# Mamba layer, then attention with experts, on one core: an earlier second front, late gates bridged by the pair's last outputs, and the net's norms and sums moved off VectorE

## The chip, the cores and the metric

One NeuronCore of a Trainium2 chip runs the whole program. The metric is the time of one execution on the device in microseconds (us), as a median over runs. The core's engines are TensorE (PE; its weight loads are listed as PEld), VectorE (DVE), ScalarE (ACT), GpSimd (POOL) and SyncE (SP). Each works through its own instructions in order, and they wait for one another through semaphores. DMAs are issued from SP and from POOL. A DMA that adds to its destination is issued from POOL here.

## The reference

The input is x, 8 sequences of 512 positions and 256 features, all in float32. Two layers follow each other:

```python
x = x + layernorm(mamba(layernorm(x)))
x = x + layernorm(ffn(layernorm(x)))

# mamba: 512 inner channels, 16 states
xs, z = split(x @ in_proj_w.T)
xc = silu(causal_conv4(xs) + conv_b)
dt_r, B, C = split(xc @ x_proj_w.T)
dt = softplus(dt_r * dt_proj_w + dt_proj_b)
h_t = exp(dt_t * A) * h_(t-1) + dt_t * B_t * xc_t        # along the sequence
y = sum over states of h * C + xc * D
return (y * silu(z)) @ out_proj_w.T

# ffn: 16 heads of width 64; 8 experts, the best 2 of each head are kept, for values and for outputs
q, k = rope(x @ Wq), rope(x @ Wk)
gv, go = gates(x, Wsel_v), gates(x, Wsel_o)              # sigmoid, top 2 of 8
v = sum_e gv_e * (x @ Wv_e);  o = softmax(q k^T / 8) @ v
src = x + sum_e go_e * (o @ Wo_e)
y = ln(src) * ln1_g + ln1_b
y = y + relu(y @ W1 + b1) @ W2 + b2
return ln(y) * ln2_g + ln2_b
```

## The kernel before

The 8 sequences, b = 0 to 7, are a pipeline. For each there are four pieces of work, written as Python generators:

- `front(b)` normalizes x, projects it, makes the convolution on VectorE (`xs`, one `tensor_scalar` and three `scalar_tensor_tensor` for each of four channel blocks), applies Silu, projects to B, C and dt, writes the gate `sz` to DRAM, and makes the softplus in pieces: `u` = exp(-|.|), `ln` = log(1 + u), and a correction that uses `w` = (1 + u) - 1, where VectorE takes u - w and adds it to `ln`. At its end b is in `prepared`.
- `mamba(b)` makes `dt` and `dtx`, then 32 scan steps. A step is a product `h<-bt,dtx`, a `tensor_tensor_scan` `h<-da,h`, and a product `h<-h,ct`, all on 128x1024, on VectorE. ScalarE makes the decay `da` of the next step in one of two buffers (`decays`), and two adding DMAs from POOL sum h into `xc` (`xc<-h`). After the scan come `xc*sz`, the output projection `ps_out`, two norms (`x1`, `xn`), the transposes `ps_tr_g`, the gate logits `ps_sel` and the first half of the gates, `best(0, gv)`. Now b is in `state`.
- `heads(b)` makes the second half of the gates, `best(1, gt)`, and writes it to DRAM (`ps_go`). Now b is in `gated`.
- `feed_forward(b)` is what the change calls the net: residual, norm, W1, Relu, W2, two norms, output.

The attention of a sequence is an order written out by hand in `ahead`, for 8 pairs of heads. For a pair there are values `ps_v` (with gates applied on VectorE and added up on POOL as `ve`), scores `ps_s`, transposes `ps_pt` and the sum `ps_o`. The eight output steps of the pair before, `last.add_output(0..7)` (matmuls `ps_a`), are spread between these. Late in each pair `follow` projects the next pair's q and k (`ps_qk`); VectorE then makes `sin` and `qk`, and four small adding DMAs from POOL (`qk<-sin`) complete the rotation that the first `ps_s` needs. At a pair 7, `follow` runs the planner until b + 1 is in `state`.

`_Order` is the planner. It keeps a clock for PE and one for VectorE, and holds the running generators with a rank; a lower rank goes first. A generator's part is emitted when VectorE's planned clock is behind PE's. A `yield` gives the estimated time until the next part can run. The planner only fixes the order in which each engine meets its instructions. `_Vector` records every VectorE instruction, so they all carry line 160 in the profile.

PSUM has three tiles of two banks for everything (`banks`) and one for the sum `ps_a`. SBUF pools `big` (7 buffers) and `half` (5) hold the temporary tiles.

Lines that matter: front(1) is started by mamba(0) with rank `FIRST` = 0.2, behind mamba(0)'s own rank 0, and holds before its convolution until `through` has 0:

```python
            while b == 1 and 0 not in through:
                yield 1.0
...
                order_of.start(front(b + 1), 2 * b - 1 if b else FIRST)
```

In the net, each half of the hidden layer is made as two tiles of two halves. TensorE makes one half, ScalarE applies Relu to it, then TensorE makes the other half of the same tile.

Of the kernel before, what the change touches and what calls it, by code (L numbers as in the profile page):

```python
# [37 lines left out]
NG = 2  # L38
# [14 lines left out]
NET, FIRST = -9, 0.2  # L53
# [8 lines left out]
class _Norm:  # L62
# [7 lines left out]
    def __call__(self, out, rows):  # L70

        nc, vector, n = self.nc, self.vector, len(rows)
        st = self.pool.tile([P, n, 6], F32, tag="ln_st", name="ln_st")
        mv = self.pool.tile([P, n, 2], F32, tag="ln_mv", name="ln_mv")
        rs = self.pool.tile([P, n], F32, tag="ln_rs", name="ln_rs")
        for i, r in enumerate(rows):
            vector.bn_stats(st[:, i, :], r)
            vector.bn_aggr(mv[:, i, :], st[:, i, :])
            yield 0.0
        vector.tensor_scalar(rs, mv[:, :, 1], EPS, None, ALU.add)  # L80
        nc.gpsimd.tensor_tensor(rs, rs, self.power[:, :n], ALU.pow)
        yield 1.5
        for i, r in enumerate(rows):
            vector.tensor_scalar(
                out[:, i, :], r, mv[:, i, 0:1], rs[:, i : i + 1], ALU.subtract, ALU.mult
            )
            yield 0.1
# [113 lines left out]
def _layers(  # L201
# [4 lines left out]
    with ExitStack() as ctx:  # L206
# [18 lines left out]
        sz_d = [tc.dram_tile([NC // 2, P, 2, S], F32, name=f"sz_d_{b}") for b in range(B)]  # L225
        wqk_d = [tc.dram_tile([P, 2, ND, P], F32, name=f"wqk_d_{i}") for i in range(H // 2)]
# [9 lines left out]
        rows_t = const.tile([P, 4, D], F32, name="rows_t")  # L236
        g1, o1, g2, o2 = (rows_t[:, i : i + 1, :].to_broadcast([P, NT, D]) for i in range(4))
# [12 lines left out]
        def later_constants():  # L250
# [5 lines left out]
            nc.sync.dma_start(out=b1_t, in_=b1)  # L256
            nc.sync.dma_start(
                out=rows_t.rearrange("p r d -> p (r d)"),
                in_=rows[:, : 4 * D].to_broadcast([P, 4 * D]),
            )  # L260
            yield 8.0

# [31 lines left out]
        def front(b):  # L294
# [43 lines left out]
            while b == 1 and 0 not in through:  # L338
                yield 1.0
# [51 lines left out]
            for u in us:  # L391
# [5 lines left out]
                for i in range(2):  # L397
                    w = half.tile([P, S], F32, tag="half", name=f"w_{b}_{m + i}")
                    vector.tensor_scalar(w, u[:, i, :], 1.0, 1.0, ALU.add, ALU.subtract)
                    yield 0.0  # L400
                    vector.tensor_tensor(u[:, i, :], u[:, i, :], w, ALU.subtract)
                    yield 0.0
                vector.tensor_tensor(ln, ln, u, ALU.add)
# [9 lines left out]
        def mamba(b):  # L413
# [3 lines left out]
            xs, lns, row = prepared[b]  # L417
            dt = one.tile([P, NC, S], F32, tag="dt", name=f"dt_{b}")
# [5 lines left out]
            for m in range(0, NC, 2):  # L424
# [4 lines left out]
                yield 0.1  # L429
            while b and b - 1 not in through:  # L430
# [5 lines left out]

            def decays(k):
                g, m = k // NC * NG, k % NC
                for j in range(NG):
                    nc.scalar.activation(  # L440
                        das[k % 2][:, j, 1:S], dt[:, m, 1:S], AF.Exp,
                        scale=decay[:, m, g + j : g + j + 1],
                    )
# [7 lines left out]
            if b + 1 < B:  # L451
                order_of.start(front(b + 1), 2 * b - 1 if b else FIRST)
                order_of.start(mamba(b + 1), 2 * (b + 1))
            steps = NS // NG * NC
            decays(0)
# [33 lines left out]
            while 0 < b < B - 1 and b + 1 not in prepared:  # L489
# [322 lines left out]
        def feed_forward(b, pa):  # L812

            xt, _ = state.pop(b)
            acc = big.tile([P, ND, S], F32, tag="big", name=f"acc_{b}")
            vector.tensor_tensor(acc, xt, pa, ALU.add)
            summed.add(b)
            yield 0.1
# [11 lines left out]
            yield from norm(y, [y[:, t, :] for t in range(NT)])  # L830
            vector.tensor_tensor(y, y, g1, ALU.mult)
            yield 0.0
            vector.tensor_tensor(y, y, o1, ALU.add)
            yield 0.1
            yt = big.tile([P, ND, S], F32, tag="big", name=f"yt_{b}")
            to_features(yt, y, f"f_{b}")
            pe(1.05)
            yield 1.2
            b2 = half.tile([P, 1, D], F32, tag="half", name=f"b2_{b}")
            nc.sync.dma_start(out=b2[:, 0, :], in_=rows[:, 4 * D :].to_broadcast([P, D]))  # L840
            vector.tensor_tensor(y, y, b2.to_broadcast([P, NT, D]), ALU.add)

            for k in range(2):
# [3 lines left out]
                for f in range(0, NF // 2, 2):  # L847
                    ps = banks(f"ps_f1_{b}_{k}_{f}")
                    h = big.tile([P, 2, S], F32, tag="big", name=f"hid_{b}_{k}_{f}")
                    for i in range(2):  # L850
                        at = k * NF // 2 + f + i
# [5 lines left out]
                        pe(1.71)  # L857
# [17 lines left out]
                yield 0.1  # L875
                vector.tensor_tensor(y, y, ps, ALU.add)
                yield 4.0
            z = big.tile([P, NT, D], F32, tag="big", name=f"z_{b}")
            x1 = big.tile([P, NT, D], F32, tag="big", name=f"x1_f_{b}")
            nc.sync.dma_start(out=x1, in_=x1_d[b])  # L880
            yield from norm(z, [y[:, t, :] for t in range(NT)])
# [4 lines left out]
            yield from norm(z, [z[:, t, :] for t in range(NT)])  # L886
            vector.tensor_tensor(z, z, x1, ALU.add)
# [9 lines left out]
        def follow(b, pair):  # L897

            b, pair = (b, pair + 1) if pair + 1 < H // 2 else (b + 1, 0)
            if b < B:  # L900
                order_of.run(lambda: b in state)
# [20 lines left out]
        with tc.manual_schedule(engines=MANUAL):  # L922
# [9 lines left out]
            for b in range(B):  # L932
                for pair in range(H // 2):
                    now = pairs.pop((b, pair))
                    ahead(now, lambda: follow(b, pair))
                    if pair == 0 and b:
# [5 lines left out]
            for k in range(E):  # L942
                last.add_output(k)
                order_of.run()
            order_of.start(feed_forward(B - 1, sums[B - 1]), NET)
# [84 lines left out]
```

## Time and profile before

| what | value |
|---|---|
| median of 3 runs (lowest to highest) | 3809.67 us (3799.65 to 3812.99) |
| the profiled execution: its time, its span | 3804.05 us, 3802.3 us |
| mean granted TensorE clock | 0.942 |
| busy in the span: PE, DVE, ACT, POOL | 88%, 80%, 44%, 44% |
| bytes moved by DMA | 584.19 MB, mean 154 GB/s |
| shares of the chain that ended last | PE 57%, DVE 21%, DMA 7%, ACT 6%, issue 6%, POOL 3% |

The profile is of one execution. "Busy" is the share of the span in which an engine had an instruction in work. The chain that ended last is followed back from the last instruction to what released it. Idle time of an engine that is not the bottleneck costs nothing. In a group of instructions, the columns are busy time and mean duration, then the idle time of that engine just before them and what ended it.

### The profile page before, as it was taken

How to read it: one execution, taken by the hardware profiler on the slowest of the kernel's cores; microseconds unless marked ns; L12 is line 12 of the kernel's file. 1: busy time of each engine (PE TensorE's matmuls, PEld its weight loads, DVE VectorE, ACT ScalarE, POOL GpSimd, SP SyncE). 2: the span in 40 equal slices, each digit the busy share in tenths (PEclk: the TensorE clock that was granted, in tenths of full speed). 3: DMA queues.
4: the chain of work that ended last, by engine and by line, in shares of the span. 5: the costliest groups of instructions: out<-in, count | busy, mean ns of one | idle time of the engine just before them, and what ended most of it. 6: DMA issues, size and time to landing. Idle time of an engine off the chain costs nothing.

```text
span 3802.3 us, 33611 instructions
## 1 busy us (share of the span) xinstructions
PE 3362.9 (88%) x10464; PEld 1560.0 (41%) x10464; DVE 3049.0 (80%) x3218; ACT 1657.2 (44%) x2761; POOL 1656.8 (44%) x1601
## 2 busy tenths in 40 slices
PE   2039999399989999999999999999999999999996
PEld 0023444244444444444444444444444444444443
DVE  6976899799879888799878988799888989664432
ACT  4216654144544446444563446334463435332331
POOL 1323466255534545345443554445453557332220
PEclk6569999699999999999999999999999999999998
DMA  5934778368755867468674877557683777443431
GB/s 164 202 63 128 176 188 194 84 168 192 179 146 139 189 168 192 119 160 195 160 187 106 195 173 190 141 145 187 162 208 91 182 193 180 116 111 101 120 94 56
DMA packets 287760, 584.19 MB, mean 154 GB/s; under 512 B 37848, under 2 KB 125144, under 8 KB 287584
## 3 DMA queue, kind: packets, MB, share of 16 engines
q1 hardware_dynamic: 205664, 431.00, 38.3%
q0 software_dynamic: 81920, 151.04, 24.5%
q8 instruction: 85, 1.39, 0.1%
q14 instruction: 91, 0.75, 0.1%
HBM read 409.39 MB, written 21.51 MB: 113 GB/s over the span
## 4 chain that ended last, share of the span: by engine, by line
PE 57%; DVE 21%; DMA 7%; ACT 6%; issue 6%; POOL 3%; SPq 0%; DVEq 0%; POOLq 0%; ACTq 0%
PE ps_a L803 16%; PE ps_v L735 14%; DVE h L160 8%; PE ps_s L676 5%; PE ps_o L764 3%; PE ps_pt L711 3%; PE ps_f L853 3%; DMA xc<-h 3%; PE ps_qk L638 3%; PE ps_f L868 3%; DVE og L160 2%; DMA qk<-sin 2%; DVE ve L160 2%; PE ps_out L511 2%; DVE low L160 1%
## 5 line engine op out<-in xcount | busy, mean ns | idle before, releaser
L750 POOL TENSOR_TENSOR ve<-ve 128x512 f32<-128x512 f32 x256 | 420.2, 1641 | 1348.6 <-DVE ve L160 1248.0
L803 PE MATMUL ps_a<-og,wo 128*128 128x512 f32 x2048 | 978.5, 617 | 11.6 <-DVE og L160 11.2
L735 PE MATMUL ps_v<-wv,xt 128*128 128x512 f32 x2048 | 935.2, 599 | 3.8 <-ACT p L691 3.8
L160 DVE TENSOR_TENSOR_SCAN h<-da,h 128x1024 f32<-128x1024 f32 x256 | 609.7, 2382 | 87.1 <-ACT da L440 74.5
L691 ACT ACTIVATE p<-ps_s,low 128x512 f32<-128x512 f32 x512 | 347.3, 683 | 708.2 <-DVE low L160 707.7
L448 POOL DMA_DIRECT2D xc<-h x512 | 493.3, 1168 | 360.0 <-DMA xc<-h 145.6
L803 PEld LDWEIGHTS ps_a<-og,wo 128*128 128x128 f32 x2048 | 378.7, 195 | 547.4 <-issue 471.9
L735 PEld LDWEIGHTS ps_v<-wv,xt 128*128 128x128 f32 x2048 | 380.5, 191 | 517.0 <-issue 472.8
L700 ACT ACTIVATE p<-p,total 128x512 f32<-128x512 f32 x512 | 341.2, 714 | 190.5 <-DVE total L160 190.5
L160 DVE TENSOR_TENSOR og<-o,gb 128x1024 f32<-128x1024 f32 x256 | 311.6, 1238 | 118.2 <-ACT o L770 49.5
L160 DVE TENSOR_TENSOR ve<-ps_v,gv 128x1024 f32<-128x1024 f32 x256 | 311.4, 1216 | 117.4 <-PE ps_v L735 113.6
L717 ACT COPY pt<-ps_pt 128x1024 f32<-128x1024 f32 x256 | 256.7, 1003 | 334.8 <-PE ps_pt L711 334.1
L676 PE MATMUL ps_s<-qk 64*128 64x512 f32 x1024 | 328.8, 660 | 82.4 <-DMA qk<-sin 60.1
L440 ACT ACTIVATE da<-dt,decay 128x511 f32<-128x511 f32 x512 | 337.6, 713 | 140.9 <-DVE h L160 140.4
L160 DVE TENSOR_TENSOR h<-bt,dtx 128x1024 f32<-128x1024 f32 x256 | 345.1, 1348 | 17.6 <-DMA xc<-h 17.3
L160 DVE TENSOR_REDUCE low<-ps_s 128x2 f32<-128x1024 f32 x256 | 310.8, 1214 | 56.8 <-PE ps_s L676 55.9
L160 DVE TENSOR_TENSOR h<-h,ct 128x1024 f32<-128x1024 f32 x256 | 326.2, 1274 | 3.6
L751 POOL TENSOR_TENSOR ve<-ve 128x256 f32<-128x256 f32 x256 | 308.1, 1203 | 20.2
L660 POOL DMA_DIRECT2D qk<-sin x256 | 207.9, 1258 | 214.1 <-DVE qk L160 85.1
L711 PEld LDWEIGHTS ps_pt<-ident,p 128*128 128x128 f32 x2048 | 240.2, 142 | 133.9 <-issue 106.3
L711 PE MATMUL ps_pt<-ident,p 128*128 128x128 f32 x2048 | 267.5, 274 | 6.2 <-ACT pt L717 6.1
L511 PE MATMUL ps_out<-w_out,xc 128*128 128x256 f32 x256 | 66.5, 422 | 213.5 <-DVE xc L160 211.6
(114 smaller groups left out, 3271.9 us busy)
## 6 DMA issues: line engine op xcount, KB each, us to landing
xc<-h POOLq DMA_DIRECT2D x512, 256.0 KB, 5.7
gb<-go_d SPq DMA_DIRECT2D x512, 256.0 KB, 5.0
wv<-in_wv_dram SPq DMA_DIRECT2D x128, 512.0 KB, 4.6
wo<-in_wo_dram SPq DMA_DIRECT2D x512, 128.0 KB, 3.6
bt<-bc_d SPq DMA_DIRECT2D x64, 512.0 KB, 6.2
ct<-bc_d SPq DMA_DIRECT2D x64, 512.0 KB, 7.1
wqk<-wqk_d SPq DMA_DIRECT2D x64, 256.0 KB, 2.6
qk<-sin POOLq DMA_DIRECT2D x256, 64.0 KB, 4.4
```

Source lines behind the costliest of these rows:

```text
L160: return getattr(self.engine, name)(*args, **kw)
L440: nc.scalar.activation(das[k % 2][:, j, 1:S], dt[:, m, 1:S], AF.Exp, scale=decay[:, m, g + j : g + j + 1],)
L448: nc.gpsimd.dma_start(out=xc[:, k % NC, :], in_=h[:, j, :], accum_op=ALU.add)
L676: nc.tensor.matmul(ps[:, j, :], lhsT=self.qk[feats, 0, bass.ts(t, P)], rhs=self.qk[feats, 1, :], start=True, stop=True,)
L691: nc.scalar.activation(p[:, j, :], ps[:, j, :], AF.Exp, bias=low[:, j : j + 1], accum_out=total[:, j : j + 1],)
L700: nc.scalar.mul(p[:, j, :], p[:, j, :], total[:, j : j + 1])
L711: nc.tensor.transpose(pp[:, j, bass.ts(i, P)], self.p[t][:, j, bass.ts(i, P)], ident)
L717: nc.scalar.copy(self.pt[:, :, :, bass.ts(t, P)], pp.rearrange("p j (i q) -> p j i q", q=P))
L735: nc.tensor.matmul(ps[:, i, :], lhsT=self.xt[:, c, bass.ts(t + i, P)], rhs=self.wv[:, c, :], start=(c == 0), stop=(c == ND - 1),)
L750: nc.gpsimd.tensor_tensor(ve[:, :, 0:4], ve[:, :, 0:4], ve[:, :, 4:8], ALU.add)
L751: nc.gpsimd.tensor_tensor(ve[:, :, 0:2], ve[:, :, 0:2], ve[:, :, 2:4], ALU.add)
L803: nc.tensor.matmul(pa[:, c, :], lhsT=self.wo[:, i, bass.ts(c, P)], rhs=self.og[q][:, i, :], start=(self.pair == 0 and k == 0), stop=(self. ...
```

## The change

It has five parts.

1. **The second front.** front(1) is started with rank -1, before mamba(0)'s 0, and no longer waits for `through`. mamba(0) waits after its scan until front(1) is prepared, as the others did. The first decays of a sequence, `decays(0)`, are emitted right after dt and dtx and ahead of the wait for `through`.
2. **Late gates.** `follow` no longer runs the planner until b + 1 is in `state`; if it isn't, nothing is projected. After pair 7 is attended, and if pair 0 of b + 1 has not been projected, the eight output steps of pair 7 are emitted at once, with a try of `follow` after each. The net of b starts then, and pair 0 of b + 1 has no output steps between its parts.
3. **The net's norms.** ScalarE applies them as scale * x + offset, with one small VectorE instruction for the offset. The softplus's `w` = 1 + u is also made on ScalarE, and VectorE does one `scalar_tensor_tensor` in place of two instructions.
4. **The net's sums.** ScalarE copies out of PSUM, and an adding DMA from POOL adds: the residual, b2 (together with ln1_b, laid out in DRAM at the start), both halves of W2's product, and x1 at the end. ln1_b's own addition goes into the copy of `yt` as ScalarE's bias.
5. **Relu.** Both halves of a hidden tile are made before ScalarE applies Relu to the two.

```diff
-    def __call__(self, out, rows):
+    def __call__(self, out, rows, scalar=None):
...
+        if scalar:
+            off = self.pool.tile([P, n], F32, tag="ln_off", name="ln_off")
+            vector.scalar_tensor_tensor(off, mv[:, :, 0], -1.0, rs, ALU.mult, ALU.mult)
+            yield 0.1
+            for i, r in enumerate(rows):
+                scalar.activation(
+                    out[:, i, :], r, AF.Identity, scale=rs[:, i : i + 1], bias=off[:, i : i + 1]
+                )
+                yield 0.5
+            return
...
-            while b == 1 and 0 not in through:
-                yield 1.0
...
-                    vector.tensor_scalar(w, u[:, i, :], 1.0, 1.0, ALU.add, ALU.subtract)
+                    nc.scalar.activation(w, u[:, i, :], AF.Identity, bias=1.0)
+                    yield 0.9
+                    vector.scalar_tensor_tensor(
+                        u[:, i, :], w, -1.0, u[:, i, :], ALU.add, ALU.subtract
+                    )
                     yield 0.0
-                    vector.tensor_tensor(u[:, i, :], u[:, i, :], w, ALU.subtract)
-                    yield 0.0
-                vector.tensor_tensor(ln, ln, u, ALU.add)
+                vector.tensor_tensor(ln, ln, u, ALU.subtract)
...
+            decays(0)
             while b and b - 1 not in through:
                 yield 0.5
...
-                order_of.start(front(b + 1), 2 * b - 1 if b else FIRST)
+                order_of.start(front(b + 1), 2 * b - 1)
...
-            while 0 < b < B - 1 and b + 1 not in prepared:
+            while b + 1 < B and b + 1 not in prepared:
                 yield 0.5
...
         def feed_forward(b, pa):
+            def add_to(t, what):
+                nc.gpsimd.dma_start(out=t, in_=what, accum_op=ALU.add)
...
-            vector.tensor_tensor(acc, xt, pa, ALU.add)
+            nc.scalar.copy(acc, pa)
+            yield 1.2
+            add_to(acc, xt)
...
-            yield from norm(y, [y[:, t, :] for t in range(NT)])
+            yield from norm(y, [y[:, t, :] for t in range(NT)], nc.scalar)
             vector.tensor_tensor(y, y, g1, ALU.mult)
-            vector.tensor_tensor(y, y, o1, ALU.add)
...
+            for c in range(ND):
+                nc.scalar.activation(yt[:, c, :], ps[:, c, :], AF.Identity, bias=o1[:, c : c + 1])
+            add_to(y, ob_d.rearrange("o t d -> o (t d)").to_broadcast([P, NT * D]))
...
                     for i in range(2):
-                        at = k * NF // 2 + f + i
                         for c in range(ND):
                             nc.tensor.matmul(...)
-                        pe(1.71)
+                    pe(3.42)
+                    for i in range(2):
+                        at = k * NF // 2 + f + i
                         nc.scalar.activation(
                             h[:, i, :], ps[:, i, :], AF.Relu, bias=b1_t[:, at : at + 1]
                         )
...
-                vector.tensor_tensor(y, y, ps, ALU.add)
+                part = big.tile([P, NT, D], F32, tag="big", name=f"part_{b}_{k}")
+                nc.scalar.copy(part, ps)
+                yield 1.2
+                add_to(y, part)
...
-            yield from norm(z, [z[:, t, :] for t in range(NT)])
-            vector.tensor_tensor(z, z, x1, ALU.add)
+            yield from norm(z, [z[:, t, :] for t in range(NT)], nc.scalar)
+            add_to(z, x1_d[b])
...
         def follow(b, pair):
             b, pair = (b, pair + 1) if pair + 1 < H // 2 else (b + 1, 0)
-            if b < B:
-                order_of.run(lambda: b in state)
+            if b in state and (b, pair) not in pairs:
                 pairs[b, pair] = Pair(b, pair)
                 pairs[b, pair].project()
...
                     last = now
-            for k in range(E):
-                last.add_output(k)
-                order_of.run()
-            order_of.start(feed_forward(B - 1, sums[B - 1]), NET)
+                if (b + 1, 0) not in pairs:
+                    for k in range(E):
+                        last.add_output(k)
+                        order_of.run()
+                        follow(b, pair)
+                    order_of.start(feed_forward(b, sums[b]), NET)
+                    last = None
+                if b + 1 < B:
+                    order_of.run(lambda: b + 1 in state)
+                    follow(b, pair)
```

In the order of the built program, the outputs of pair 7 go first at the ends of sequences 0 to 5. At the end of sequence 6 pair 0 has been projected in time, and the order is the old one.

## The prediction

> **What bounds the kernel now.** I first read the table of stages, cut where the work changes. Its columns are the stage, its length, then the busy time (with counts) of PE, PEld, DVE, ACT and POOL, the granted clock, the DMA share and GB/s.
>
> ```profile
> 0.00:282.60 282.60, 57.80 (x145) 29.54 (x145) 220.66 (x225) 87.99 (x117) 64.72 (x90) 0.62 0.61 144
> 282.60:650.00 367.40, 348.56 (x1043) 151.27 (x1044) 304.90 (x286) 200.66 (x326) 186.71 (x171) 0.97 0.70 171
> 650.00:800.00 150.00, 85.46 (x261) 44.15 (x260) 125.99 (x136) 48.93 (x83) 58.05 (x48) 0.75 0.49 113
> 800.00:3700.00 2900.00, 2804.15 (x8805) 1299.81 (x8804) 2366.72 (x2516) 1304.02 (x2214) 1339.34 (x1286) 0.98 0.65 158
> 3700.00:3802.30 102.30, 66.92 (x215) 35.28 (x213) 30.74 (x57) 15.59 (x24) 7.93 (x9) 0.86 0.17 53
> ```
>
> The change leaves TensorE's work as it is, so the time moves with TensorE's idle time: 224.8 us before the first scores, 18.8 in the first attention, 64.5 where attention passes from sequence 0 to 1, 95.9 in the 2900 after, 35.4 in the tail; 439.4 of 3802.3. The first stage belongs to VectorE (221 of 283). Next, who ends TensorE's waits from 650 to 800:
>
> ```profile
> PE ps_out L511 <- DVE xc L160: 26.3, 2, 22.7
> PE ps_tr_g L282 <- DVE xn L160: 23.9, 1, 23.9
> PE ps_s L676 <- DVE top L160: 13.2, 1, 13.2
> ```
>
> These are sequence 1's scan, its norms and its gates, one behind the other (total, times, longest). The timeline of a later passage (start, duration, what, wait) shows the small form of the same thing:
>
> ```profile
> 2060.54 3.70 PE L735 MATMUL ps_v<-wv,xt 128*128 128x512 f32 x8
> 2068.42 3.91 PE L676 MATMUL ps_s<-qk 64*128 64x512 f32 x4 [4.18 <-DMA qk<-sin]
> 2072.26 4.90 PE L803 MATMUL ps_a<-og,wo 128*128 128x512 f32 x8
> 2080.52 1.13 PE L676 MATMUL ps_s<-qk 64*128 64x512 f32 x4
> ```
>
> A pair 0 waits 4.2 us for its rotation, and what follows runs slowly: 3.91 where 1.13 is usual, 4.90 for 3.70. Last, the waits of the whole run for Relu, and in the tail the outputs right behind `ps_o`:
>
> ```profile
> PE ps_f L853 <- ACT hid L858: 25.3, 32, 1.2
> ...
> 3720.91 7.13 PE L803 MATMUL ps_a<-og,wo 128*128 128x512 f32 x16 [1.94 <-DVE og L160]
> ```
>
> **The change, part by part** (plus is slower).
>
> *First scan, +27.* front(1) puts onto VectorE, ahead of the scan's end, its norm (2.4 for statistics, 1.4 to apply), the convolution (four of 0.54, twelve of 0.77: 11.4) and the softplus (four `scalar_tensor_tensor`, by the 769 ns row, and two sums of 1.245: 5.6). That is 21, and VectorE is busy 144.6 of the 150 us from 50 to 200, so nothing hides it. ScalarE (57 of 150) and the idle TensorE hide theirs. Then a new wait. In the built order, two scan steps of sequence 1 stand ahead of x1's statistics. The second needs a decay that ScalarE makes behind the copy of `ps_out` (ends 234.3) and four products `xc` (2.6): 234.3 + 2.6 + 1.3 + 2.3 for the scan itself = 240.5 instead of 234.3, so +6.2. The statistics and the whole chain to the first `ps_s` queue behind it. dt and dtx (5 us) fit into the wait for the last adding DMAs (216.9 to 222.8). Convolution in front of the first rotation (4.2) gives way to reciprocals (3.4). Sum 27; bounds 21 (the wait hidden) and 33 (decays held by the added table loads of 1.28).
>
> *TensorE's share of front(1), -11.* `ps_x` 3.55 and two `ps_in` of 3.65 and 3.71 leave the first attention for idle time.
>
> *Passage 0 to 1, 64.5 to 20.5: -44.* By the built order and the rows' durations, VectorE has 284 us of work instead of 339 between the first rotation and sequence 1's `xc*sz`: softplus 7.9, dt and dtx 5, four scan steps 20, reciprocals 3.4, most of a pair. From 350 to 650 it was busy 89%, so 284 / 0.89 + 8 for the last sums = 327. TensorE's work up to `ps_out` falls from 338 to 297, which at the 380 / 338 of before is 334, and with less of its first-pair loss about 325. The two meet; I keep 7 of the 26.3 (0 to 26). `ps_tr_g` now stands behind some 37 us of pair 7, more than the 24 it waited: 0. From the end of `ps_sel` to the first `ps_s` the gates took 28; outputs, `ps_qk` and `ps_v` (13.7 + 3.4 + 3.4) now cover 20.6: 7.5 left. Pair 0 without outputs: the only such pair in the trace idled 0.24 + 1.63 + 3.49 + 1.48 = 6.8; I take 6.
>
> *Slow running behind those waits, -5.* Here `ps_s` took 3.67 (1.13), `ps_a` 5.42 (3.70), `ps_tr_g` 2.21 (1.04), some 9 with `ps_out`; I take about half (0 to -9).
>
> On this the Trainium skill, "TensorE: Matmul & The Clock Gate", section "What's actually happening", says that a clock gate halves the rate after an idle window of about 3.4 us and lets go after as much work. By it, a gap costs at most 1.7 us, so this term would be about -3, and idle in smaller pieces would cost nothing more. The clock row agrees in kind (0.75 in this stage, 0.98 later).
>
> *Relu after both halves, -22.* Of the 25.3, 3.2 are in the tail. The next matmul writes another tile, so nothing takes its place. Bounds -22 and -15.
>
> *Passages 1 to 5, +10.* Before, each cost 4.2 + 2.8 + 1.2 = 8.2. Now outputs cover the rotation, but `ps_a` stands directly behind `ps_o`: in the tail 1.94 + 0.30 = 2.2. VectorE's `og` stands behind half a gate chain: 1.5 more. The pair without outputs: 6.5. That is 10.2, +2 for each of five. Bounds: only 2.2 (-30 in all), or the 13.7 of outputs lost whole (+39).
>
> *Adding DMAs, +6 outside the tail.* 35 of 512 KB join POOL's queue. A late one, or a ScalarE copy it waits for, holds back `ve` sums, `xc` sums and the four rotation DMAs issued behind it. Outside the passages rotations cost TensorE 60.1 - 22.1 - 23.6 = 14 us, beside 448 adds: by that row 2 us more, with twice the size. One rotation held per sequence by a full add and the slow restart would be 7 x (4.7 + 2.8) = 52. I stay near the row.
>
> *VectorE relieved, -3.* The net loses 13.2 us per sequence (norms 5.6, sums 7.6) and the softplus 2.4, against 0.6 for offsets: 120 in all. VectorE ends few of TensorE's waits after 800, so nearly all of it is idle time there; bounds 0 and -20. ScalarE takes some 12 more per sequence, at 44% busy; its exponents queue behind, priced in the passages.
>
> *Tail, +10.* An add of 256 KB lands after 3.3 us there; 512 KB is estimated from it at 4.7 (the transfer part doubled). Residual and second half: 1.02 + 4.7 for 1.22, +4.5 each. x1: +3.5. Norms on ScalarE: +0.6 each, 1.8. Gone: ln1_b's 1.24 and Relu's 3.2. Bounds 4 and 16.
>
> The Trainium skill, "DMA: Bandwidth & Descriptors", section "Anatomy of one DMA", prices one at 2.0 us plus bytes over 436 GB/s. The trace's 3.3 for 256 KB is above its 2.6; by it, an add of 512 KB takes 3.2 and the tail comes to +6. It speaks against trading a 1.2 us VectorE sum on a chain for a DMA, as the row does.
>
> Sum: 27 - 11 - 44 - 5 - 22 + 10 + 6 - 3 + 10 = -32. The profiled execution's 3804.05 us (span and 1.75 around it) becomes 3772; it stands 5.6 below the median, so beside the median: 3809.67 - 32 = 3778.
>
> **Rivals.**
> *The passage stays late: 3806.* VectorE fell 22 us behind its place in the order before 662 and may again; `ps_out` (26.3) and gates (13.2) then stay, and only `ps_tr_g`'s wait goes: +25.5, and +3 of slow running. For it: the first scan pays its 27 in any case. Against: 55 us less work.
> *Slower: the stripped pair 0, 3838.* The outputs are filler. If the softmax chain and VectorE's order set pair 0's length, all 13.7 us are lost instead of 6 to 6.5, and the idle brings a slow restart of 2.8, in six passages: 60 more. It turns the sign from 5.3 us a passage beyond my figure. For it: four waits in the trace's only such pair. Against: its longest, 3.5, was for the gates, and two gaps came with front(1)'s table loads.
> *More: 3740.* `ps_out` doesn't wait, and pairs without outputs idle hardly at all: -7 and -30.
> That the change doesn't do what it says is excluded by the built order.
>
> **How the numbers follow.** Forecast 0.46 (own range 3758 to 3797), more gain 0.14, passage late 0.17, slower 0.23. A run of this kernel can be told from no change by about 0.3%, 11.4 us. Faster than 3798: nearly all of the forecast, 0.45, the 0.14, and a little of the late case, 0.04: 0.63. Within: 0.13, the late case. Slower: 0.24. The range reaches from 3740 to 3832: below lies half of the more-gain case, above half of the slower one.
>
> **What would show it.** Right: first `ps_s` near 309; idle from there to sequence 1's first pairs near 20 beyond the small waits; no waits of `ps_f` for `hid`; a tail some 10 longer; VectorE near 2930 us busy. Wrong: a wait of 20 or more at `ps_out`; gaps in every pair 0 adding to over 13 us; `ps_s` waiting for `qk<-sin` behind an adding DMA of the net; a first scan longer by over 33.

## The result, and the profile after

The changed kernel takes 3869.87 us (3867.19 to 3872.13, 4 runs) beside 3804.66 for the kernel before on the same chip: a ratio of 1.0174, interval 1.0156 to 1.0192. It is slower by 65 us where 32 us of gain were forecast.

The stages of the changed kernel (stage, length, busy time of PE, PEld, DVE, ACT and POOL, clock, DMA share, GB/s), the first cut at the first scores:

```profile
0.00:314.80 314.80, 73.56 (x168) 35.40 (x169) 250.78 (x249) 121.82 (x162) 71.97 (x95) 0.63 0.63 151
650.00:800.00 150.00, 129.30 (x404) 60.36 (x401) 119.62 (x147) 55.56 (x100) 55.09 (x56) 0.93 0.50 120
800.00:3700.00 2900.00, 2734.82 (x8562) 1272.86 (x8561) 2241.00 (x2351) 1339.34 (x2289) 1320.98 (x1292) 0.98 0.67 160
```

The passage from sequence 0 to 1 is mended: TensorE works 129 of its 150 us, not 85. But in the 2900 us after, TensorE idles 165 us and not 96, while VectorE works 126 us less there (111 less in the whole run). Cut at the start of `ps_o` of a sequence's pair 0, from the two traces (and, for later, from that of the best experiment):

| stretch | before | after | parts 1 and 5 alone |
|---|---|---|---|
| start to b = 0 | 330.0 | 345.1 | 351.3 |
| b = 0 to 1 | 471.0 | 424.2 | 420.9 |
| b = 1 to 6, five sequences | 2180.5 | 2254.4 | 2139.8 |
| b = 6 to 7 | 401.5 | 405.3 | 396.8 |
| b = 7 to the end | 419.4 | 437.6 | 413.8 |

Up to b = 1 the change is ahead by 31.7 us. The five steady sequences then lose 73.9, the end 18.2. Beyond the first scan, TensorE's waits of the whole run (total, times, longest) show no single large loss:

```profile
PE ps_a L831 <- DVE og L172: 52.7, 26, 4.2
PE ps_o L792 <- ACT pt L745: 20.0, 10, 4.5
PE ps_pt L739 <- ACT p L728: 19.9, 11, 3.6
PE ps_f L891 <- DMA w<-in_w_dram: 14.2, 4, 4.8
```

Before, these were 11.2, 3.6, nearly nothing and 0.3 us in total; the 25.3 us of `ps_f` for `hid` are gone. A later passage in the timeline (start, duration, what, wait), the counterpart of the one shown for before:

```profile
2069.78 3.65 PE L792 MATMUL ps_o<-pt,v 128*64 128x512 f32 x16
2076.84 3.53 PE L831 MATMUL ps_a<-og,wo 128*128 128x512 f32 x4 [3.40 <-DVE og L172]
2080.16 3.79 PE L666 MATMUL ps_qk<-xt,wqk 128*128 128x512 f32 x8
2083.78 5.31 PE L831 MATMUL ps_a<-og,wo 128*128 128x512 f32 x12
...
2101.76 1.13 PE L704 MATMUL ps_s<-qk 64*128 64x512 f32 x4
...
2109.86 1.27 PE L739 MATMUL ps_pt<-ident,p 128*128 128x128 f32 x8 [2.28 <-ACT p L728]
...
2130.45 3.65 PE L792 MATMUL ps_o<-pt,v 128*64 128x512 f32 x16 [1.19 <-ACT pt L745]
```

`ps_s` no longer waits for its rotation. In exchange `ps_a` waits 3.40 us behind `ps_o`, and its next four matmuls take 3.53 where 1.88 is usual; then come the gaps of a pair without outputs. And in the tail:

```profile
3771.52 7.13 PE L831 MATMUL ps_a<-og,wo 128*128 128x512 f32 x16 [1.95 <-DVE og L172]
3779.09 7.11 PE L831 MATMUL ps_a<-og,wo 128*128 128x512 f32 x16 [0.43 <-DMA wo<-in_wo_dram]
3792.21 1.94 PE L860 MATMUL ps_acc<-ident,acc 128*128 128x128 f32 x8 [6.02 <-DMA acc<-xt]
```

The third line is the net's residual: it now waits 6.02 us for an adding DMA, where the kernel before waited 1.31 for VectorE. From the last `ps_a` (3786.2) to the end (3866.6) are 80.4 us, 66.8 before.

### The profile page after: what moved, and what is told of

The parts are those of the page before. It is cut to its first block, busy times and chain, and to the rows that moved or that the text cites. A ratio compares the mean times of both kernels' runs of the same rounds, so it can differ in the third digit from the quotient of the medians.

```text
span 3866.6 us, 33716 instructions
## 1 busy us (share of the span) xinstructions
PE 3372.2 (87%) x10464; PEld 1564.8 (40%) x10464; DVE 2938.3 (76%) x3067; ACT 1731.1 (45%) x2915; POOL 1663.6 (43%) x1641
## 5 line engine op out<-in xcount | busy, mean ns | idle before, releaser
L831 PE MATMUL ps_a<-og,wo 128*128 128x512 f32 x2048 | 967.0, 611 | 59.4 <-DVE og L172 52.7
L763 PE MATMUL ps_v<-wv,xt 128*128 128x512 f32 x2048 | 951.5, 608 | 12.5 <-ACT p L719 10.0
L172 DVE TENSOR_TENSOR og<-o,gb 128x1024 f32<-128x1024 f32 x256 | 322.3, 1279 | 165.2 <-DMA gb<-go_d 76.7
L704 PE MATMUL ps_s<-qk 64*128 64x512 f32 x1024 | 314.9, 661 | 65.4 <-DMA qk<-sin 40.0
L792 PE MATMUL ps_o<-pt,v 128*64 128x512 f32 x1024 | 240.7, 612 | 20.2 <-ACT pt L745 20.0
```

Source lines behind the costliest of these rows:

```text
L172: return getattr(self.engine, name)(*args, **kw)
L704: nc.tensor.matmul(ps[:, j, :], lhsT=self.qk[feats, 0, bass.ts(t, P)], rhs=self.qk[feats, 1, :], start=True, stop=True,)
L763: nc.tensor.matmul(ps[:, i, :], lhsT=self.xt[:, c, bass.ts(t + i, P)], rhs=self.wv[:, c, :], start=(c == 0), stop=(c == ND - 1),)
L792: nc.tensor.matmul(po[j * HP : j * HP + HP, 0, :], lhsT=self.v[:, j, t, :], rhs=self.pt[:, j, t, :], start=(t == 0), stop=(t == NT - 1),)
L831: nc.tensor.matmul(pa[:, c, :], lhsT=self.wo[:, i, bass.ts(c, P)], rhs=self.og[q][:, i, :], start=(self.pair == 0 and k == 0), stop=(self. ...
```

## The experiments

All were timed beside the kernel before (medians 3802 to 3804 us). "Price" is a difference of medians between kernels with and without a piece; the runs of one kernel spread by 4 to 20 us, so prices below about 10 us aren't told from nothing. First, parts are taken back from the changed kernel; then, parts are put on the kernel before. Where a piece lies in the course of the program is read from one trace for each kernel.

### One part taken back from the changed kernel

**Part 2 taken back**: the hunks in `follow` and after the pair loop are reversed.

```diff
-            if b in state and (b, pair) not in pairs:
+            if b < B:
+                order_of.run(lambda: b in state)
...
```

> The changed kernel with part 2 taken back: pair 7's outputs are spread through pair 0 again, and projecting waits for the gates as before. Between the two profiles TensorE's idle time (counted from one ps_o of a pair 0 to the next) rose by 9.8, 5.2, 20.7, 4.9 and 18.1 us in the sequences from pair 0 of b = 1 to pair 0 of b = 6: 59 us. Theory 'outputs': this is the filler taken out of pair 0 and the outputs set directly behind ps_o, so it goes with part 2: 3870 - 59 = 3811, plus up to 10 for gates that are bare again. Theory 'sums': the net's adding DMAs and ScalarE copies do it, and this kernel stays within 10 us of 3870. Theory 'ScalarE': the norms and copies there hold the exponents back; it stays within 10 us of 3870 too.

3805.93 us, ratio 1.0001 (0.9988 to 1.0014): 64 us come back. Part 2 is the largest cost of the three taken back here; the change without it takes what the kernel before takes.

**Part 4 taken back**: `vector.tensor_tensor(acc, xt, pa, ALU.add)` and its like in place of each `add_to`.

> The changed kernel with part 4 taken back: all of the net's sums (residual, ln1_b, b2, both halves of W2's product, x1) are VectorE's again, with no adding DMA in the net. Theory 'sums': the 59 us of idle time in the steady sequences and the 13 us of the longer tail go: about 3800. Theory 'outputs': only the tail's adds go, 8 to 13 us: 3857 to 3862. Theory 'ScalarE': two of the five moved pieces of work leave ScalarE, so about a third of the 59 and the tail's 10: some 3840.

3856.39 us, 1.0142 (1.0123 to 1.0161): 14 us, what the tail lost; from the last `ps_a` to the end are 66.2 us again. The theory of the sums falls as the main cause.

**Part 3 taken back**: `norm(...)` without `nc.scalar`, and `w` and u - w on VectorE.

> The changed kernel with part 3 taken back: the net's three norms are applied by VectorE and the softplus's correction is two VectorE instructions again. Theory 'ScalarE': the exponents and copies of the softmax no longer queue behind 12 applications and 4 copies a sequence: two thirds of the 59 us, about 3830. Theories 'outputs' and 'sums': VectorE has room, so within 10 us of 3870; 2 us off for the tail, up to 2 us on in the first scan for the softplus.

3822.41 us, 1.0053 (1.0036 to 1.0070): 48 us, as the theory of ScalarE had it. But 64 + 14 + 48 is more than the 65 us lost: the parts either share their cost, or parts 1 and 5 gain much. Part 3's two halves, `w` taken back first, then the norms:

```diff
-                    nc.scalar.activation(w, u[:, i, :], AF.Identity, bias=1.0)
+                    vector.tensor_scalar(w, u[:, i, :], 1.0, 1.0, ALU.add, ALU.subtract)
```

> The changed kernel with only the softplus's correction taken back: w = (1 + u) - 1 and u - w are two VectorE instructions again; the net's norms stay on ScalarE. Taking back both pieces of part 3 gave 3822, 48 us less than 3870. In the changed kernel's profile VectorE stood idle 78.1 us in 17 waits for ScalarE's w (52.6 in 14 waits after 800 us). Theory 'round trip': VectorE stands in its order for an instruction that ScalarE has queued behind others, and softmax, gates and outputs queue behind it; this half of part 3 is most of the 48 us: 3825 to 3838. Theory 'norms': the 12 applications of norms a sequence, each waiting for offsets from VectorE and POOL, hold ScalarE's exponents back: this kernel stays at 3860 to 3870.

```diff
-            yield from norm(y, [y[:, t, :] for t in range(NT)], nc.scalar)
+            yield from norm(y, [y[:, t, :] for t in range(NT)])
```

> The changed kernel with only the net's three norms taken back to VectorE; the softplus's w stays on ScalarE. Theory 'round trip': 3855 to 3868, only the tail's 2 us and small waits. Theory 'norms': 3825 to 3838. If the two pieces hinder each other by filling the same queue, both this kernel and the one with the softplus alone taken back give about half of the 48 us: 3845.

3852.16 us (1.0132, 1.0112 to 1.0151) and 3857.60 us (1.0147, 1.0131 to 1.0162): 18 and 12 us, and 48 only together. Neither theory alone holds.

**Only some outputs first**: in the changed kernel, outputs stop as soon as pair 0 is projected.

```diff
+                        last.given = k + 1
                         follow(b, pair)
+                        if (b + 1, 0) in pairs:
+                            break
```

> The changed kernel, except that at the end of a sequence outputs of pair 7 are emitted only until pair 0 of b + 1 can be projected; the others are spread through pair 0 as before. In the changed kernel's profile, at the ends of sequences 1 to 5 the order is four matmuls of ps_a (one output), then ps_qk, then the other 28 of ps_a: the gates are late by one output, and seven more go at once. Theory 'outputs' (pair 0 without filler): of the 64 us that taking part 2 back gave, 45 to 60 come: 3810 to 3825, and the bridge at the end of sequence 0, where all eight are used, stays. Rival 'the wait moves': ps_a still stands directly behind ps_o for its first og (4 us a passage) and pair 0 is short of one output; 20 to 30 us come: 3840 to 3850.

3886.72 us, 1.0223 (1.0202 to 1.0245): 17 us slower still, against both theories. The order is one output, then `ps_qk`, `ps_v` and `ps_s`: without outputs behind `ps_qk` nothing covers the rotation, and `ps_s` waits for it longer. First the changed kernel, then this one (each has 21.4 before the first scores):

```profile
PE ps_s L704 <- DMA qk<-sin: 40.0, 13, 21.4
PE ps_s L704 <- DMA qk<-sin: 79.3, 24, 21.4
```

### Parts on the kernel before

**Relu alone** (part 5):

> The kernel before with part 5 alone: both halves of a hidden tile, then Relu. The prediction's term: the waits of ps_f for hid, 25.3 us in 32 waits, go and nothing takes their place: -22, about 3783. Rival 'the wait moves on': the second projection or the next pair's work then waits for the two Relus behind each other (0.6 us later per tile) and the order around it shifts; the gain is under 8 us: 3797 to 3807.

3788.28 us, 0.9954 (0.9933 to 0.9975): by the ratio -17, between -25 and -10; the prediction's -22 lies within.

**Parts 1 and 5:**

> The kernel before with parts 1 and 5 alone (the earlier second front, Relu after both halves): no outputs first, no work on ScalarE or by adding DMAs. By the prediction's terms: first scan +27, TensorE's share of the front -11, passage 0 to 1 -44 less what part 2 gave there (gates 13.2 to 7.5 and the 6 of the stripped pair, about even), slow running -5, Relu measured at -14 to -18 alone: 3802 - 33 - 16 = 3753. The changed kernel with part 2 taken back measured 3806, with part 3 taken back 3822 and with part 4 taken back 3856; if what the parts cost adds up, 3870 - 64 - 48 - 14 = 3744. Rival 'shared waits': parts 2 and 3 remove the same waits, so taking both back gives little more than one: 3780 to 3795.

3720.24 us (3717.37 to 3724.34), 0.9782 (0.9766 to 0.9798). This beats the kernel before by 83 us and the changed one by 150, below every expectation. Part 1 mends the passage from 0 to 1 without part 2: from b = 0 to b = 1 this kernel takes 420.9 us, the changed one 424.2, and Relu alone 473.9. From here on this kernel is called the base.

**The place of `decays(0)`**, an edit of part 1 in one line:

```diff
-            decays(0)
             while b and b - 1 not in through:
...
             steps = NS // NG * NC
+            decays(0)
```

> Parts 1 and 5 (measured 3720), but the first decays of a sequence are again emitted behind the wait for through and the products xc. From the fourth sequence on, part 1 shortened a sequence by 7 to 13 us against Relu alone, though fronts from b = 2 on are untouched; the one edit of part 1 that acts there is the place of decays(0). Theory 'decays': this kernel loses that, 30 to 40 us, and up to 4 in the first scan: 3750 to 3764. Rival 'phase': the gain comes from the first passage, which sets how work falls against pairs later on: 3715 to 3730.

3774.42 us, 0.9921 (0.9896 to 0.9945): 54 us, more than the 30 to 40 expected. By the traces 16 of them lie between b = 0 and b = 1 (436.9 for 420.9) and 32 in the five steady sequences. The other edits of part 1 are then worth 14 (3788.28 to 3774.42). VectorE's waits for the decays from 700 to 3500 us, first with `decays(0)` late, then early:

```profile
DVE h L172 <- ACT da L433: 55.4, 10, 10.2
```
```profile
DVE h L172 <- ACT da L433: 18.7, 6, 7.8
```

and where that is, in VectorE's timeline, first in the kernel before, then with the decays late:

```profile
1991.98 2.29 DVE L160 TENSOR_TENSOR_SCAN h<-da,h 128x1024 f32<-128x1024 f32 x1 [7.88 <-ACT da L440]
```
```profile
1975.69 2.29 DVE L172 TENSOR_TENSOR_SCAN h<-da,h 128x1024 f32<-128x1024 f32 x1 [8.45 <-ACT da L433]
...
1980.29 0.42 DVE L172 BATCH_NORM_STATS2 ln_st<-x 128x6 f32<-128x256 f32 x1
```

The first scan step of a sequence waits 8.45 us for a decay that ScalarE makes behind a copy and four products (7.88 us in the kernel before). Behind it in VectorE's order stand the statistics of `x1` of the sequence ahead, and so its norms, gates and pair 0: pair 7, in which the gates are made, took 55.9 us with the decays late and 48.8 with them early (means of b = 1 to 5).

**Part 2 on the base:**

> Parts 1 and 5 (measured 3720) and part 2 (all outputs first where gates are late). Between the changed kernel and the one with part 2 taken back, the mean sequence from b = 1 to 5 spent 63.1 and 49.4 us up to ps_o of pair 0, 68.4 and 63.0 in pair 1, 56.5 and 70.6 in pair 2, 56.2 and 45.0 in pair 3; over all eight pairs part 2 cost some 11 us a sequence. Theory 'own price': part 2 costs this without parts 3 and 4 too, 3720 + 5 x 11 - 6 (the wait of 16.6 at passage 0 to 1 falls to 10.0) = 3769; at the most the 64 that taking it back gave, 3784. Rival 'only in company': pair 0 without filler is bad only because ScalarE and POOL are late, 3715 to 3730.

3832.80 us, 1.0072 (1.0047 to 1.0098): 113 us. A passage of it, first TensorE's, then VectorE's timeline:

```profile
2033.79 3.65 PE L776 MATMUL ps_o<-pt,v 128*64 128x512 f32 x16 [0.73 <-ACT pt L729]
2037.37 3.72 PE L554 MATMUL ps_sel<-w_sel,xt 128*128 128x256 f32 x16
...
2076.77 3.64 PE L688 MATMUL ps_s<-qk 64*128 64x512 f32 x4 [13.18 <-DMA qk<-sin]
2080.34 5.14 PE L747 MATMUL ps_v<-wv,xt 128*128 128x512 f32 x8
```
```profile
2066.96 3.38 DVE L172 RECIPROCAL s<-s 128x128 f32<-128x128 f32 x4
2070.26 1.16 DVE L172 TENSOR_TENSOR sin<-ps_qk,angle 128x1024 f32<-128x1024 f32 x1
```

Even the logits `ps_sel` now come behind `ps_o` of pair 7, at every passage from 0 to 5; in the base they come before it. Nothing holds the planner to the gates any more, so they are late by the change's own making, which the next kernel tests. Outputs, `ps_qk` and `ps_v` cover 22 us of it, then `sin` stands behind the whole gate chain on VectorE and `ps_s` waits 13.18.

**Outputs first, but the gates forced as before:**

```diff
-            if b in state and (b, pair) not in pairs:
+            if b < B and (b, pair) not in pairs:
+                order_of.run(lambda: b in state)
...
-                if (b + 1, 0) not in pairs:
+                if True:
```

> Parts 1 and 5 (measured 3720) and one half of part 2: all eight outputs of pair 7 go at once behind ps_o, and pair 0 runs without outputs, but the planner still runs until b + 1 is in state within pair 7, so the gates and ps_qk stand where they stood before. All of part 2 on this base measured 3833, +113. Theory 'late by its own making': the price is that nothing holds the planner to the gates, so ps_sel and ps_qk come behind ps_o of pair 7 and ps_s of pair 0 waits 13 us in every passage (87.9 us in 16 waits with all of part 2); with gates where they were, only ps_a's wait behind ps_o (2 to 4) and small gaps in pair 0 are left, 3 to 6 a passage in seven: 3740 to 3762. Rival 'stripped pair 0': a pair without filler costs it whatever the gates do: 3800 to 3833.

3776.03 us, 0.9922 (0.9903 to 0.9941): 56 us instead of 113, between the two theories' ranges; each has half. With the gates early, it is `og` that stands behind them:

```profile
2033.50 3.65 PE L776 MATMUL ps_o<-pt,v 128*64 128x512 f32 x16
2043.46 9.62 PE L815 MATMUL ps_a<-og,wo 128*128 128x512 f32 x16 [6.31 <-DVE og L172]
```
```profile
2041.59 0.68 DVE L172 TENSOR_REDUCE top<-key 128x64 f32<-128x512 f32 x1
2042.19 2.35 DVE L172 TENSOR_TENSOR og<-o,gb 128x1024 f32<-128x1024 f32 x2
```

An output that is to cover the gates needs a product that VectorE makes, and VectorE is at the gates. At the passage from 0 to 1 the same wait is 23.66 us. From the traces, means of the sequences b = 1 to 5, length and, in brackets, TensorE's gaps over 0.3 us (cut at the ends of `ps_o`):

| kernel | pair 0 | pairs 1 to 4 | pairs 5 to 7 | sequence |
|---|---|---|---|---|
| before | 52.1 (5.4) | 227.0 (4.3) | 158.7 (8.5) | 437.8 (18.2) |
| changed | 63.1 (10.1) | 241.7 (14.8) | 147.8 (5.8) | 452.6 (30.7) |
| changed, part 2 back | 49.4 (4.5) | 239.9 (16.2) | 151.9 (4.4) | 441.2 (25.1) |
| parts 1, 5 | 54.0 (6.3) | 226.3 (2.4) | 150.1 (5.2) | 430.4 (13.9) |
| parts 1, 5, 2 | 73.7 (17.4) | 229.3 (5.6) | 142.9 (5.8) | 445.9 (28.8) |
| the same, gates forced | 66.1 (15.0) | 224.8 (4.2) | 149.2 (4.5) | 440.1 (23.7) |

Pair 0 is where part 2 costs. A little of its length is only work moved there from pair 7: `ps_qk` (3.8 us) in the changed kernel, `ps_qk` and `ps_sel` (3.7) with parts 1, 5 and 2, and pairs 5 to 7 are shorter by about as much. The gaps of pairs 1 to 4 are there without part 2, and come with parts 3 and 4.

**Part 2 at the end of sequence 0 alone:**

```diff
+            if b > 1 and b < B:
+                order_of.run(lambda: b in state)
             if b in state and (b, pair) not in pairs:
```

> Parts 1 and 5 (measured 3720) and part 2 at the end of sequence 0 alone; at the others the planner runs until the gates are there, as before. Theory 'own making': at the one passage where gates are late in any case, ps_s waits 16.6 us, and with part 2 in full 10.0; part 2 gains there 4 to 8: 3712 to 3716. Rival: pair 0 and pair 1 without filler give it back: 3719 to 3726.

3742.20 us, 0.9832 (0.9816 to 0.9848): 22 us slower, against both. The profiled execution took 3731.49 us, so its trace holds about half of this. At that passage `ps_s` waits 13.27 instead of 16.58, but waits of `ps_go` (2.57) and `ps_a` (3.98) are new. And the next passage, which had nothing changed, now has the wait that this one was to lose:

```profile
1171.70 3.72 PE L688 MATMUL ps_s<-qk 64*128 64x512 f32 x4 [16.55 <-DMA qk<-sin]
```

It took 64.9 us up to `ps_o` of its pair 0 (start to start), 48.5 on the base. By this reading the lateness isn't covered but handed on. Part 2 has no passage where it was seen to pay.

**Part 3 on the base**, then `w` alone, then the norms alone:

> Parts 1 and 5 (measured 3720) and part 3 (norms and the softplus's w on ScalarE). Taken back from the changed kernel its halves gave 18 and 12 us, both 48. Theory 'own price': 30 to 48, 3750 to 3768, with VectorE idle some 70 us for w. Rival 'only in company': with outputs spread over pair 0, ScalarE's delay is hidden: 3715 to 3730.

> Parts 1 and 5 (measured 3720) and of part 3 only the softplus's w on ScalarE. Both halves together measured 3746 on this base, +25. Theory 'round trip': VectorE, waiting in order for w, gives the larger half: +13 to +25, 3733 to 3745. Rival 'norms': the norms on ScalarE give it, and w alone costs at most the 1 or 2 us of the first scan: 3718 to 3725.

> Parts 1 and 5 (measured 3720) and of part 3 only the net's norms on ScalarE. Both halves gave 3746, w alone 3721. If prices add, the norms are the +25: 3740 to 3750. If the two halves cost only together (w and norms meet in ScalarE's order in the same pairs): 3718 to 3728.

3745.63 us (0.9851, 0.9828 to 0.9873), 3720.75 us (0.9781, 0.9766 to 0.9795) and 3738.99 us (0.9824, 0.9805 to 0.9843): 25 us, nothing and 19 us. On the base the theory of the round trip falls: with `w` on ScalarE VectorE waits,

```profile
DVE u L172 <- ACT w L410: 39.9, 15, 3.8
```

and it costs no time. The norms do. TensorE's waits from 650 to 3500 us with the norms on ScalarE, then on the base:

```profile
PE ps_s L688 <- ACT p L703: 28.3, 26, 2.5
PE ps_f L870 <- DMA w<-in_w_dram: 27.7, 6, 5.4
```
```profile
PE ps_s L688 <- ACT p L703: 2.4, 9, 0.7
PE ps_f L869 <- DMA w<-in_w_dram: 1.0, 1, 1.0
```

Scores wait for exponents that ScalarE makes late, and W1 for its weights. Which of the two makes the 19 us isn't shown: with part 4 alone, the next kernel, W1 waits 37.0 us for its weights and the time doesn't grow. Why the weights' load comes late wasn't tried.

**Part 4 on the base**, then without the last sequence's sums:

> Parts 1 and 5 (measured 3720) and part 4 (the net's sums by adding DMA). Theory 'tail only': what taking it back from the changed kernel gave, 14 us: 3734. Theory 'the net comes late': with outputs spread over pair 0, the kernel with part 2 taken back idled 5.1 us a sequence at ps_f and 1.9 at ps_acc in pair 1, where this base idles 0.2 and 0; 7 a sequence in seven, and 14 in the tail: 3720 + 49 + 14 = 3783.

3722.92 us, 0.9793 (0.9769 to 0.9816): no price. By the trace the steady sequences gain 5 us each, sequence 6 loses 6, and the stretch from b = 7 to the end loses 19 (433.2 for 413.8), 13 of them behind the last `ps_a`.

```diff
+            if b == B - 1:
+                vector.tensor_tensor(acc, xt, pa, ALU.add)
```

> Parts 1 and 5 (measured 3720) and part 4, except that the last sequence's residual, product halves and x1 are summed by VectorE (ln1_b and b2 are VectorE's in every sequence). With part 4 on this base the five steady sequences took 422.8 us instead of 428.0 in the mean and the last 404.7 from its ps_o of pair 0 instead of 395.0, 3723 in all. Theory 'the tail pays for the steady part': without the tail's adds 3700 to 3713. Rival: the steady gain is one of order (where ps_f and ps_acc fall), and goes when b2 and ln1_b return to VectorE: 3718 to 3730.

3771.70 us, 0.9916 (0.9900 to 0.9932): 49 us above the kernel with all of part 4, where a gain or no change was expected. The stretch from b = 7 got 15 us shorter, but the steady sequences took 434 us and not 423, though only ln1_b and b2 differ there. What this order costs, and why, stays open.

**Parts 1, 4, 5 and `w`**, the pieces without a price:

> Parts 1, 4 and 5 and w on ScalarE: all of the change but part 2 and the norms, the pieces that cost nothing by themselves on this base (part 4: 3723, w: 3721). If prices add: 3718 to 3726. If VectorE's relief counts once both pieces are moved, 3700 to 3715; if the waits for w (40 us of VectorE) and for the net's adds meet, 3735 to 3760.

3758.65 us, 0.9866 (0.9842 to 0.9890): 38 us from two pieces that cost nothing singly. `ps_out` waits now, 16.8 us instead of 6.2 with part 4 alone, and pair 6 takes 65.1 us and not 57.5 in the mean of five sequences, which is the whole price. The waits of W1 for its weights are no longer than with part 4 alone. First with part 4 alone, then this kernel, from 650 to 3500 us:

```profile
PE ps_f L887 <- DMA w<-in_w_dram: 37.0, 12, 5.3
...
PE ps_out L536 <- DVE xc L172: 6.2, 6, 1.5
```
```profile
PE ps_f L890 <- DMA w<-in_w_dram: 34.6, 11, 4.6
...
PE ps_out L539 <- DVE xc L172: 16.8, 6, 3.3
```

All eight combinations of parts 2, 3 and 4 on the base have been measured (medians in us):

| added to parts 1 and 5 | without part 2 | with part 2 |
|---|---|---|
| nothing | 3720 | 3833 |
| part 3 | 3746 | 3856 |
| part 4 | 3723 | 3822 |
| parts 3 and 4 | 3806 | 3870 |

Parts 2 and 3 add up: 113 and 25 singly, 136 together. Parts 3 and 4 don't: 25 and 3 singly, 86 together. With part 2 there, part 4 on top of part 3 costs 14, without it 60. `w` and part 4 alone make 38 of the 86. Why parts 3 and 4 hinder each other isn't shown; the gaps of pairs 1 to 4 (16.2 us a sequence for both, 2.4 on the base) are where it is seen. The best version found is parts 1 and 5.

## Why the prediction was wrong, point by point

*First scan, share of the front, passage 0 to 1, slow running: 27 - 11 - 44 - 5 = -33.* Right: -31.7 at `ps_o` of b = 1. The first `ps_s` stood at 314.8 (309 forecast, bound kept), `ps_out` waited 1.4. But the credit is part 1's; what I gave part 2 there comes without it. And some of it is luck: by the traces 16 us of this passage hang on `decays(0)`, for which the sum had no term.

*The price of `decays(0)`: none given.* This is the largest thing missed on the good side. I counted dt and dtx into a wait of the first scan and wrote that VectorE ends few of TensorE's waits. The page of before had the scan's own line with 87.1 us of idle time, ended by `da` for 74.5:

```profile
L160 DVE TENSOR_TENSOR_SCAN h<-da,h 128x1024 f32<-128x1024 f32 x256 | 609.7, 2382 | 87.1 <-ACT da L440 74.5
```

Waits of 8 to 12 us, one at the end of each sequence from 0 to 5, make up most of that, and they are on the path through the gates to the passage. One line of the change was worth 54 us on the base.

*Relu, -22.* Right in kind; -17 measured, the `hid` waits gone.

*Passages 1 to 5, +10.* **The step that failed.** It is part 2's price: 64 us when taken back from the changed kernel, 113 on the base. Its pieces were not too small. At the outputs `ps_a` behind `ps_o` 3.7 us of waiting were forecast and 4.2 measured, in the rest of the stripped pair 6.5 forecast and 4.6 measured (means of passages 1 to 5). The comparison was wrong. The 8.2 of the old order held 4.0 of slow running (2.8 and 1.2), the 10.2 of the new one none. By gaps alone, pair 0 had 5.4 us before and 10.1 after (b = 1 to 5), and slow running behind the new gaps comes on top: with part 2 taken back a sequence got 11.4 us shorter, of which 5.6 are gaps and, by an estimate from TensorE's busy time at a granted clock of 0.50 in the two traces, some 3.7 slow running. That is +57 for five, not +10; 64 in the medians. On the base it is more, since there the gates come wholly behind `ps_o`.

Behind it lies a wrong picture. I took the gates for late in all passages. They were late in one. Elsewhere the planner's run until `state`, which part 2 takes out, had put them in time, or nearly. And I took the outputs for filler that lacks little: 1.5 us for an `og` behind half a gate chain. `og` is VectorE's and stands behind the same gates; with the gates at their old place it made `ps_a` wait 6.31.

*VectorE relieved, -3; ScalarE's exponents "priced in the passages".* **This failed too.** Wrong sign: part 3 costs 25 us on the base, 48 with the others. The exponents had no term at all: the passages' 2.2, 1.5 and 6.5 hold none for ScalarE. I went by its busy share (44%). With the net's norms on it, scores waited 28.3 us for exponents on the base instead of 2.4, and the busy share shows nothing of that.

*Adding DMAs, +6, tail +10.* About right for the whole change: 14 come back without them, the tail grew by 13.6. An add of 512 KB was estimated at 4.7 us for the tail and landed there after 4.5 to 5.3; over the whole run its four kinds took 6.1 to 7.8 in the median. The estimate was partly lucky: the 3.3 us of a 256 KB add that it starts from were read at the end of the first scan (216 to 224 us), not in the tail, and no run splits them into a fixed and a transfer part. What the sum lacks is part 4 beside part 3: 60 us without part 2.

*The rivals.* The slower one named the right part and mechanism ("VectorE's order set pair 0's length") at 3838. With its 60 us more, part 2 costs some 70, near the 64 measured when it is taken back; it was too small because it kept -3 for part 3. Of the marks listed, nearly all came as forecast (first scores, no `hid` waits, VectorE at 2938, gaps in pair 0 under 13 but for the 14.9 of passage 0 to 1, a tail 14 longer), and the difference of the two profiled executions was still 96 us off (+64 for -32): none of the marks looked at pairs 1 to 4, where gaps grew from 4.3 to 14.8 a sequence.

In all, parts 1 and 5 brought 83 us where 55 were forecast, and parts 2 to 4 cost 150 on top of them where 23 were.

## What to carry to other kernels

Before filler is moved to cover a late chain, see which engine makes the filler's inputs: if it is the engine of the late chain, nothing is covered. Compare an old stall and a new one in the same coin, idle time and slow running both, and count the whole period of a pipeline. Before work is moved to an engine with a low busy share, see what stands behind it there. Where one in-order planner serves several engines, price a part by itself on the chip and then with the others: parts that cost 113, 25 and 3 us alone but 64, 48 and 14 when taken back, and two that cost nothing singly and 38 together, can't be summed on paper.

## What the runs showed of the hardware

The slow running goes with TensorE's granted clock. Windows of the traces in which it was 0.50 throughout (window, length, busy time of PE, PEld, DVE, ACT and POOL, clock, DMA share, GB/s), in the changed kernel twice, in the kernel before, with the gates forced twice, and with parts 1, 5 and 2:

```profile
2077.12:2080.53 3.41, 3.41 (x5) 1.36 (x5) 3.28 (x5) 0.00 (x0) 0.00 (x0) 0.50 0.68 180
2111.25:2114.67 3.42, 3.42 (x12) 1.92 (x11) 1.30 (x2) 1.40 (x3) 0.14 (x1) 0.50 0.63 195
```
```profile
2067.88:2074.71 6.83, 6.29 (x7) 2.17 (x8) 6.76 (x9) 0.00 (x0) 0.54 (x1) 0.50 0.34 81
```
```profile
1604.77:1611.60 6.83, 3.35 (x4) 1.51 (x5) 5.13 (x7) 0.00 (x0) 0.00 (x0) 0.50 0.39 93
2041.67:2048.50 6.83, 5.04 (x6) 2.19 (x7) 3.47 (x5) 0.00 (x0) 0.00 (x0) 0.50 0.55 142
```
```profile
2066.21:2083.28 17.07, 6.51 (x8) 2.39 (x9) 10.53 (x14) 1.45 (x4) 5.65 (x7) 0.50 0.13 16
```

In the first, four `ps_a` took 3.53 us where 1.88 is usual. The windows are one, two and five times 3.41 us long. They stand at waits of 3.40, 2.28, 4.18, 6.32, 6.31 and 13.18 us, and TensorE worked 3.4, 3.4, 6.3, 3.4, 5.0 and 6.5 us in them at half the clock. So even 2.28 us of idle time brought slow running, and what it costs doesn't follow the length of the wait: twice 6.3 us had 3.4 and 5.0 us of slow work behind them, and 4.18 us almost as much as 13.18.

The Trainium skill's page "TensorE: Matmul & The Clock Gate", section "What's actually happening", puts the return to full rate at about 3.4 us of sustained work, which from half rate is an estimated 1.7 us lost. The changed kernel's two windows agree with that. Behind 4.18 and 13.18 us the half rate lasted for 6.3 and 6.5 us of work, about 3.2 us lost each time.

Adding DMAs of 512 KB landed after 6.1 to 7.8 us in the median over the changed kernel's run, those of 256 KB (`xc<-h`) after 6.2. In the tail, from 3780 us on, where the DMA share is 0.27 and not 0.65 as in the mean, the ones of 512 KB took 4.5 to 5.3. So the same 512 KB took 1.4 to 2.8 us longer in the median of the whole run, and two of their four kinds were no slower there than 256 KB.
